# A graph-attention and mixture-of-experts kernel: the last batch of ten edge tiles becomes two batches, of six and of four

## The chip, the core and the metric

The kernel runs on one core of one Trainium2 chip. The metric is device time in microseconds (us) of one execution; the smaller the better. The core has five engines with a queue of instructions each: TensorE (PE, matrix products, with its weight loads shown as PEld), VectorE (DVE), ScalarE (ACT), GpSimd (POOL, here the issuer of indirect DMAs) and SyncE (SP, here the issuer of the plain DMAs). Each engine works its queue in order; semaphores make it wait for others. Sixteen DMA engines move data between HBM and the on-chip memory.

## The reference

The input is a graph of 6250 nodes (256 features each) and 100000 edges, sorted by destination. Two layers follow each other, each with a residual.

```python
x = x + gnn(layernorm(x), [src, dst], edge_attr_2, W_forward, W_reverse, attn)
x = x + ffn(layernorm(x), gate_w, gate_b, w1, b1, w2, b2)

# gnn: one message per edge, four heads, softmax over the edges of a destination
messages = h_fwd[src] * direction[:, 0:1] + h_rev[src] * direction[:, 1:2]
scores   = leaky_relu(einsum('ef,hf->eh', messages, attn))
norm     = exp(scores - max) / (segment_sum(exp(...), dst)[dst] + 1e-10)
out      = segment_sum(messages * norm, dst), for each head

# ffn: each token goes to the best of 8 experts (256 -> 1024 -> 256, relu), up to a capacity
idx  = argmax(softmax(x @ gate_w + gate_b));  pos = rank of the token within its expert
y    = expert(x)[idx, pos] * prob * (pos < capacity)
```

## The kernel before, in words

**Edges.** First a table of the nodes' products with the two weight matrices is written to HBM (node_tab). The 100000 edges make 782 tiles of 128 edges. The tiles are worked in batches of up to GB = 12 (two halves of GT = 6), in the order of the list `order` (L942): from the highest destination down to tile HEAD = 106, and at the end the 106 tiles of the head, which all belong to the first 128 nodes, upwards: eight batches of 12 and one of 10. That makes NB = 66 batches, numbered 0 to 65.

For each batch b:

- `gathers(b)` (L1041): POOL issues one indirect DMA per tile, which fetches the source rows into `gt` (three buffers). After the sixth tile it may put one waiting piece of POOL work (`pool_work`) between two gathers.
- `messages(b)` (L1051): DVE scales and adds the gathered rows (L1058 to L1067), makes scores (L1070), their maximum for the batch (L1074) and subtracts a shift (L1078); ACT takes the exponential (L1080).
- `places(b)` (L1083): DVE makes the 0/1 matrix `hot` (L1088) that says which of 128 destinations an edge has.
- `products(b)` (L1099): DVE multiplies messages by weights into `v` (L1103, L1104).
- `windows(b, half)` (L1117): PE adds six tiles at a time into the sums `pv` (two matmuls a tile, L1140). The 106 head tiles are summed in one `pv` without a break; after the last of them ACT copies the sums to `part_b` (L1144).

`hot`, `v`, `m` and `sc` have two buffers each. All of these and `gt` live in the pool p2.

**Routes.** The nodes are handled in 13 chunks (twelve of four tiles, the last one of the single tile 0). `route` (L1161) is a generator: once the edges of a chunk are summed, it finishes the attention, adds the residual, takes moments and normalises (L666 to L682), transposes on PE (L1201, `pt`), makes the logits (L1209, `pl`), picks the expert, counts positions with a matmul (L1231 and L1232, `pre`) and ends in `to_put` (L1256), the row to which each token is put. `put` (L1259, L1260) is the indirect DMA on POOL that writes the tokens into the experts' buffers `buf`. Early in a route the largest score so far is spread over the partitions with four transposes (`spread`, L1012 to L1017, `pm`), reduced by DVE (`over_s`) and put into the denominator.

**Experts.** Tokens are worked in four passes (`PASS`, 256, 384, 256 and 128 rows per expert); a pass can start once the chunks that belong to it are routed. The 32 jobs (24 of passes 0 to 2, then 8 of the last pass, numbered 24 to 31) form another generator, `experts` (L1385): transposes of the rows (`px`, L1335), products with the first weights (`ph`, L1409), with the second (`py`, L1426), bias and store (`y`, L1346, L1348). Rows, `w1t` and `w2t` are loaded on SP (L1320, L1297, L1305). Jobs 24 and 25 use the weights of jobs 22 and 23 again; those of 26 to 31 are fetched anew into the pool p6. The transposes of the next job come ahead of a job's `py` if that job's rows have been asked for (L1417).

**The order.** The whole order is written out by hand (manual schedule); each engine gets its instructions in the order in which the Python code issues them. The loop over b (L1505) runs NB + 1 times. Between the edge steps it takes expert steps: `step_experts(share)` (L1494) adds a half share (SHARE / 2 = 4.25) to a credit, then takes steps while the credit is positive, and each step takes off its cost, the number that the generator yields (0.86 for `px`, 1.72 for `ph`, 3.4 for `py`; the route's PE steps take off theirs as well). One turn of the loop is, in short:

```python
messages(b)
windows(b - 1, 0);  step_experts(SHARE / 2);  step_routing()
places(b);  step_routing();  products(b);  step_routing()
windows(b - 1, 1);  step_experts(SHARE / 2);  step_routing()
gathers(b + 3)
```

In turn NB - 2 the last chunk's loads are issued (L1513); in turn NB its route joins the list (L1519), so that it goes on at each `step_routing`. After the loop the pool p2 is closed and p6 takes its space (L1549, L1550). Then, in order: weights of job 26 (L1551); the rest of the last route, one step at a time, each followed by one expert step and one `fetch_and_finish` (L1555); the last put (L1559); the rows of jobs 24 and 25 and the weights of 27 and 28 (L1562 to L1566); the global check of the scores (L1571); then the expert steps that are left, with one `fetch_and_finish` after every second one (L1597); then what is left of `fetch_and_finish`, the last indirect stores, and a flag that says whether a general path has to be taken (L1610 to L1622).

`fetch_and_finish` (L1455) works on pairs of node tiles, 22 in all: it finishes the pair that was fetched four calls ago (L1374 on DVE, a store on SP, L659) and asks for the next pair (two indirect gathers `yg` on POOL, L1442, and `xr` on SP, L1446).

Of the kernel before, what the change touches and what calls it, by code (L numbers as in the profile page):

```python
# [519 lines left out]
def kernel(  # L520
# [50 lines left out]
    GB = 12  # L571

    def tiles_of(n, sign):

        u = (n / N) ** 0.5
        return (NE * u + sign * 5 * (NE * u * (1 - u)) ** 0.5) / P
# [3 lines left out]
    HEAD = int(tiles_of(P, -1)) // 2 * 2  # L580
    NL = (int(0.56 * ET) - HEAD) // GB
    GT = GB // 2
# [357 lines left out]

    assert TOP < ET and (TOP - HEAD) % GB == 0
    order = [(TOP, ET)] + [(i, i + GB) for i in range(TOP - GB, HEAD - 1, -GB)]  # L942
    order += [(i, min(i + GB, HEAD)) for i in range(0, HEAD, GB)]
    NB = len(order)
    done_at = [max(ROUTE_AT - 1, next(b for b, (i0, i1) in enumerate(order) if i0 <= groups[r][0])) for r in ready]
    done_at.append(NB - 1)
# [50 lines left out]
    with tc.tile_pool(name="p4", bufs=1) as p4, tc.tile_pool(name="p5", bufs=2) as p5, \  # L997
# [507 lines left out]
        for b in range(NB + 1):  # L1505
# [37 lines left out]
            if wait_pass and not pool_work:  # L1543
                taken["rows"] = wait_pass.pop() + 1
                i = (taken["rows"] - 1) * E
# [107 lines left out]
```

## Time and profile before

| | |
|---|---|
| median of 6 runs | 1281.58 us (1276.67 to 1283.38) |
| profiled execution | 1281.67 us, its span 1279.9 us, 14755 instructions |
| mean granted TensorE clock | 0.887 |
| PE busy | 1021.7 us (80% of the span) |
| DVE busy | 871.9 us (68%) |
| POOL busy | 864.3 us (68%) |
| ACT busy | 283.2 us (22%) |
| moved by DMA | 218.47 MB, mean 171 GB/s |
| last gather of an edge tile issued | 1136.1 us |
| last edge matmul ends, part_b is copied | 1161.4, 1161.9 us |
| the last put of the routes | 1180.1 us |
| rows of job 24 asked for | 1185.2 us |
| last expert matmul ends | 1267.1 us |

All times of single instructions count from the span's start. A line such as "PE L1140 MATMUL pv<-v,hot x12" is a run of twelve instructions of one source line; "[2.05 <-DMA xe<-buf]" says that the engine was idle for 2.05 us ahead of it and that a landing DMA ended this. In a list of waits the numbers are the total, how many times, and the longest. The shares of the whole span say little about a change at one place of a long order: the stretch in question has to be read by itself.

### The profile page before, as it was taken

The page shows a single profiled execution, that of the slowest core. Times are in us where ns is not written, and L with a number is a line of the kernel's source. Part 1 is how long each engine was busy: PE and PEld are TensorE (multiplying, and loading weights), DVE is VectorE, ACT ScalarE, POOL GpSimd, SP SyncE. Part 2 cuts the span into 40 slices and gives each one's busy share as a digit, 9 for nine tenths or more (in the row PEclk, how much of TensorE's full clock was granted, in tenths as well). Part 3 has the DMA queues.
Part 4 walks back from the last instruction along what each step waited for, and adds up shares of the span by engine and source line. Part 5 has one row for each costly group of instructions (what it writes and reads, how often), then busy time and mean ns, then how long its engine had stood idle before and what let it go on. Part 6 is the DMA issues. An engine that isn't in the chain of part 4 may idle for free.

```text
span 1279.9 us, 14755 instructions
## 1 busy us (share of the span) xinstructions
PE 1021.7 (80%) x4658; PEld 857.5 (67%) x4658; DVE 871.9 (68%) x1879; ACT 283.2 (22%) x754; POOL 864.3 (68%) x912
## 2 busy tenths in 40 slices
PE   4825555566749979797997997998999989999886
PEld 4814444455538768686876776776777878888775
DVE  6845666788828959686767768867786688664222
ACT  2510001121112232322122221222122112123222
POOL 2457777777767775767677777777777777744243
PEclk9966777677768888899998998998999999999988
DMA  8425555457355674757574663655455564646994
GB/s 273 131 69 133 140 137 143 117 135 248 105 149 172 173 216 139 216 142 203 149 217 115 183 174 98 182 148 157 142 143 156 150 207 114 202 157 243 333 378 138
DMA packets 154149, 218.47 MB, mean 171 GB/s; under 512 B 20198, under 2 KB 125963, under 8 KB 153933
## 3 DMA queue, kind: packets, MB, share of 16 engines
q1 hardware_dynamic: 121981, 142.51, 34.8%
q0 software_dynamic: 31440, 73.83, 23.3%
q10 hardware_dynamic: 640, 1.09, 0.2%
q8 instruction: 39, 0.64, 0.2%
q14 instruction: 49, 0.40, 0.1%
HBM read 160.50 MB, written 57.25 MB: 170 GB/s over the span
## 4 chain that ended last, share of the span: by engine, by line
PE 45%; DVE 18%; POOL 16%; DMA 10%; issue 8%; SPq 1%; ACT 1%; DVEq 0%; POOLq 0%; ACTq 0%
PE pv L1140 15%; POOL gt L1045 15%; PE py L1426 11%; PE ph L1409 10%; DVE v L1104 4%; DMA gt<-node_tab,srci 2%; PE pl L1209 2%; PE pn L814 2%; PE pv L1139 1%; DMA part<-sums 1%; PE pt L1201 1%; DMA buf<-hx,to_put 1%; DVE ln_st L671 1%; DVE m L1067 1%; DMA sums<-r 1%
## 5 line engine op out<-in xcount | busy, mean ns | idle before, releaser
L1045 POOL DMA_INDIRECT gt<-node_tab,srci x782 | 744.3, 952 | 246.2 <-issue 230.6
L1140 PE MATMUL pv<-v,hot 128*128 128x260 f32 x1564 | 437.0, 428 | 72.9 <-DVE v L1104 68.6
L1140 PEld LDWEIGHTS pv<-v,hot 128*128 128x128 f32 x1564 | 333.8, 217 | 139.1 <-issue 74.9
L1426 PE MATMUL py<-w2t,hf 128*128 128x256 f32 x1024 | 235.4, 384 | 0.3 <-DVE y L1346 0.3
L1409 PE MATMUL ph<-xT,w1t 128*128 128x256 f32 (+2 forms) x1024 | 234.8, 382 | 0.7 <-ACT xT L1336 0.7
L1104 DVE TENSOR_TENSOR v<-m,fixed 128x3072 f32<-128x3072 f32 (+1 forms) x66 | 218.7, 3313 | 2.3
L1426 PEld LDWEIGHTS py<-w2t,hf 128*128 128x128 f32 x1024 | 195.2, 193 | 26.9 <-DVE y L1346 0.6
L1409 PEld LDWEIGHTS ph<-xT,w1t 128*128 128x128 f32 x1024 | 176.8, 192 | 43.8 <-ACT xT L1336 1.1
L1412 ACT ACTIVATE hf<-ph,b1t 128x256 f32<-128x256 f32 (+2 forms) x256 | 108.1, 473 | 193.7 <-PE ph L1409 193.3
L1060 DVE TENSOR_TENSOR gt<-gt,fixed 128x816 f32<-128x816 f32 (+1 forms) x66 | 65.6, 994 | 102.7 <-DMA gt<-node_tab,srci 92.5
L1088 DVE TENSOR_TENSOR hot<-fixed,local 128x1536 f32<-128x1536 f32 (+1 forms) x66 | 114.1, 1729 | 0.2 <-PE pv L1140 0.2
L1346 DVE TENSOR_TENSOR y<-py,b2b 128x512 f32<-128x512 f32 (+1 forms) x40 | 23.3, 582 | 103.9 <-PE py L1426 103.9
L1442 POOL DMA_INDIRECT yg<-ybuf,to_get x44 | 42.0, 955 | 72.7 <-ACT part_b L1144 25.2
L1201 PE MATMUL pt<-ident,hx 128*128 128x128 f32 x98 | 22.6, 400 | 72.9 <-DVE hx L681 72.9
L1067 DVE TENSOR_TENSOR m<-gt,rv 128x408 f32<-128x408 f32 (+1 forms) x131 | 75.5, 576 | 4.5
L1065 DVE TENSOR_TENSOR rv<-gt,fixed 128x408 f32<-128x408 f32 (+1 forms) x131 | 76.1, 581 | 2.2
L1112 ACT COPY vl<-v 128x260 f32<-128x260 f32 x56 | 22.9, 408 | 224.0 <-DVE v L1104 101.1
L1080 ACT ACTIVATE v<-sc 128x48 f32<-128x48 f32 (+1 forms) x66 | 15.9, 242 | 254.6 <-DVE sc L1078 254.4
L1201 PEld LDWEIGHTS pt<-ident,hx 128*128 128x128 f32 x98 | 17.4, 206 | 78.2 <-DVE hx L681 28.4
L1260 POOL DMA_INDIRECT buf<-hx,to_put x49 | 49.5, 1010 | 28.6 <-issue 12.2
L1028 DVE TENSOR_REDUCE over_s<-pm 128x4 f32<-128x512 f32 x14 | 9.6, 688 | 53.6 <-PE pm L1016 53.6
L1148 ACT COPY r<-pv 128x260 f32<-128x260 f32 x86 | 31.8, 370 | 62.5 <-PE pv L1140 45.4
(206 smaller groups left out, 812.2 us busy)
## 6 DMA issues: line engine op xcount, KB each, us to landing
w1t<-in_L_ffn_w_dram SPq DMA_DIRECT2D x30, 1024.0 KB, 6.6
w2t<-in_L_ffn_w_dram SPq DMA_DIRECT2D x30, 1024.0 KB, 7.2
gt<-node_tab,srci POOLq DMA_INDIRECT x782
sums<-r SPq DMA_DIRECT2D x86, 130.0 KB, 2.1
buf<-zeros SPq DMA_DIRECT2D x16, 512.0 KB, 6.7
part<-sums SPq DMA_DIRECT2D x12, 520.0 KB, 6.1
ybuf<-y SPq DMA_DIRECT2D x24, 256.0 KB, 6.1
x_d<-hx SPq DMA_DIRECT2D x11, 512.0 KB, 3.0
```

What stands on the lines that cost most here:

```text
L1045: nc.gpsimd.indirect_dma_start(out=gts[b][:, i - i0, :], out_offset=None, in_=node_tab, in_offset=bass.IndirectOffsetOnAxis(ap=srci[:, i:i ...
L1060: nc.vector.tensor_mul(fw, fw, fac[:, 0, :n].unsqueeze(2).to_broadcast([P, n, MS]))
L1065: nc.vector.tensor_mul(rv[:, :k, :], gt[:, a0:a1, MS:ROW], fac[:, 1, a0:a1].unsqueeze(2).to_broadcast([P, k, MS]))
L1067: nc.vector.tensor_add(m[:, a0:a1, :], fw[:, a0:a1, :], rv[:, :k, :])
L1088: nc.vector.tensor_tensor(hot[:, :n, :], lane_p.unsqueeze(1).to_broadcast([P, n, P]), local[:, i0:i1].unsqueeze(2).to_broadcast([P, n, P]) ...
L1104: nc.vector.tensor_mul(v[:, :n, 0:H * O].rearrange("p n (h o) -> p n h o", h=H), m[:, :n, 0:O].unsqueeze(2).to_broadcast([P, n, H, O]), w[ ...
L1140: nc.tensor.matmul(pv, hot[:, i - i0, :], v[:, i - i0, :], start=(i == g0), stop=(i == g1 - 1))
L1201: nc.tensor.transpose(pt[:, q, d, :], h[:, n + q, d * P:(d + 1) * P], ident)
L1260: ins = nc.gpsimd.indirect_dma_start(out=bufs[p], out_offset=bass.IndirectOffsetOnAxis(ap=to_put[:, n0 + n:n0 + n + 1], axis=0), in_=hx[:, ...
L1409: nc.tensor.matmul(ph[:, f - f0, :], w1t[:, d, f * P:(f + 1) * P], xT[:, d, :S], start=(d == 0), stop=(d == DC - 1))
L1412: nc.scalar.activation(hf[:, f, :S], ph[:, f - f0, :], AF.Relu, bias=b1t[:, e * FC + f:e * FC + f + 1])
L1426: nc.tensor.matmul(py[:, j - j0, :], hf[:, f, j * P:(j + 1) * P], w2t[:, f, :], start=(f == 0), stop=(f == FC - 1))
```

## The change

The list `order` gets one entry more. Of the head's 106 tiles, the eight full batches stay; the last ten tiles, one batch (96, 106) before, become two, (96, 102) and (102, 106). NB becomes 67. The functions that work a batch are not touched; the two last batches have only a first half, so their second window returns at once (L1126).

```diff
     order = [(TOP, ET)] + [(i, i + GB) for i in range(TOP - GB, HEAD - 1, -GB)]
-    order += [(i, min(i + GB, HEAD)) for i in range(0, HEAD, GB)]
+    SHORT = (HEAD - 1) // GB * GB
+    order += [(i, i + GB) for i in range(0, SHORT, GB)]
+    order += [(i, min(i + GT, HEAD)) for i in range(SHORT, HEAD, GT)]
     NB = len(order)
```

What follows from NB moves with it: the loop has 68 turns in place of 67, with two calls of `step_experts` in each; the last chunk's loads are issued in turn 65 in place of 64, and its route joins in turn 67 in place of 66.

## Prediction

> **What bounds the kernel now.** I read the stages first (busy time by stretch), then the chain of waits, then the timeline of each engine around the edit. The edit touches only the last ten of 782 edge tiles, so only what follows about 1139 us can move.
>
> Stretches; columns: us, busy time and count of PE, PEld, DVE, ACT, POOL, then clock, DMA share, GB/s:
> ```profile
> 1140.00:1150.00 10.00, 10.00 (x50) 8.75 (x49) 7.64 (x12) 2.88 (x8) 0.00 (x0) 1.00 0.36 116
> 1150.00:1160.00 10.00, 10.00 (x50) 8.77 (x49) 0.20 (x1) 0.46 (x1) 0.00 (x0) 1.00 0.11 42
> ...
> 1162.00:1187.00 25.00, 22.39 (x112) 19.24 (x110) 14.20 (x70) 10.84 (x23) 17.16 (x18) 1.00 0.95 333
> 1187.00:1209.20 22.20, 18.13 (x116) 16.73 (x116) 5.16 (x22) 5.21 (x18) 4.17 (x5) 1.00 1.00 326
> 1209.20:1221.40 12.20, 9.15 (x51) 8.10 (x51) 2.67 (x13) 2.66 (x9) 5.11 (x7) 0.82 1.04 387
> 1221.40:1241.70 20.30, 17.73 (x101) 15.77 (x102) 5.38 (x26) 5.21 (x18) 8.13 (x9) 0.86 1.07 391
> 1241.70:1262.00 20.30, 20.30 (x138) 19.06 (x139) 7.29 (x36) 5.57 (x20) 15.24 (x17) 1.00 0.80 263
> ```
> Up to 1160 PE is full, while DMA idles and DVE has almost nothing left: the last edge tiles queue behind expert matmuls on PE. From 1162 the roles change: DMA is full for 80 us and PE waits.
>
> Waits from 1160 on (total, times, longest) and four pieces of the chain:
> ```profile
> POOL yg L1442 <- ACT part_b L1144: 25.2, 1, 25.2
> DVE over_s L1028 <- PE pm L1016: 12.8, 2, 11.8
> PE px L1335 <- DMA xe<-buf: 10.7, 4, 3.2
> ```
> ```profile
> 1159.76 1.75 PE pv L1140 x8
> ...
> 1180.06 5.13 DMA buf<-hx,to_put
> 1185.20 0.33 SPq L1320
> ...
> 1187.48 8.39 DMA w2t<-in_L_ffn_w_dram
> ```
> The switch is the end of the edges: the pool p6 (output rows, last weights) takes the space of the edge tiles, so POOL stood 25.2 us until the last edge matmul and its copy (part_b) were done. The second hinge is the one put of the last node tile: SP stood at xe<-buf until it had landed, and the weights of jobs 27 and 28 are issued behind that on SP.
>
> PE around the edit; numbers in brackets are idle time:
> ```profile
> 1153.08 2.79 PE L1140 MATMUL pv<-v,hot 128*128 128x260 f32 x12
> 1155.71 3.62 PE L1426 MATMUL py<-w2t,hf 128*128 128x256 f32 x16
> 1159.16 0.60 PE L1016 MATMUL pm<-ident,top_s 128*128 128x128 f32 x4
> 1159.60 1.92 PE L1140 MATMUL pv<-v,hot 128*128 128x260 f32 x8
> ...
> 1187.90 0.41 PE L1335 MATMUL px<-ident,xe 128*128 128x128 f32 x2 [2.05 <-DMA xe<-buf]
> ```
> The six tiles (x12) and the four (x8) stand one half share of expert work apart, and neither waits for its data.
>
> **Instructions added: about nothing.** Tiles, gathers (10) and matmuls (20) stay. The second batch adds eight DVE instructions (L1058, L1060, L1070, L1074, L1078, L1088, L1103, L1104) and one ACT (L1080, 0.24). Their fixed part comes from two shapes of one line: L1088 takes 1.749 for 1536 elements and 1.483 for 1280, so 0.15; L1104 (3.354, 2.822) gives 0.16. Eight times 0.16 is 1.3 us, in DVE's 11.81 us of idle ahead of over_s (without that cover: 1.3 us). The second batch's hot and v reuse the buffers of batch 64, free when its matmuls end at 1149.2; 0.7 and 1.2 us later they are ready, and PE wants them at 1164. The gt buffer has been free since 1114.6. The four pops of POOL work that leave with the split find an empty list now too (the last puts ran at 1083 to 1092).
>
> **Order moved: this is the cost.** One more turn of the loop puts two more half shares of 4.25 ahead of its end. I walked the credits (L1494, costs at the yields of L1385 on); both orders agree up to turn 66, where the credit is -1.08, and the walk of the old order gives the PE rows above. Old turn 66: W6, py (3.4), pm (0.9), W4, ph ph. New turn 66: W6, py, then 4.02 of credit buys ph ph ph; turn 67: W4, then 3.11 buys ph px py, then pm, then 0.48 buys one py. (W6, W4: the windows of six and four tiles.)
>
> Durations are those of the chain: py 3.45, three ph 5.18, one ph 1.73, px 0.44, pm 0.44, W4 1.75.
> 1. W4 ends at 1155.71 + 3.45 + 5.18 + 1.75 = 1166.1, before at 1161.35: the edges end **4.7 us later**. DMA, with share 0.11, has nothing to do in that time.
> 2. pm now stands behind ph px py: 1166.1 + 1.73 + 0.44 + 3.45 = 1171.7, before 1159.2. over_s to the add of part_b took 2.2 after it, and still does: 1173.9 (1161.96). The moments end 3.0 later, 1176.9. The table load for the root, which now ran at 1165.86 behind relus, has nothing ahead of it (at 1041.65 one ran 9 us ahead of its activation), so root, reciprocal and scaling take 1.1: PT at 1178.0 (1168.15), PE idle 0.7 (1.46).
> 3. The route's remaining steps fall between ph, ph, ph, py, py of job 23, where they fell between ph, px, py, py of 22: PL at 1180.0, PRE at 1183.8, to_put 2.3 after that: 1186.3 (1176.8). Job 23 ends at 1191.0.
> 4. POOL issues 14 output gathers at 1.25 ahead of the put, from 1167.0. The last pair needs the first pair's buffer: finished by DVE behind lg at 1182.7, its store lands 2.8 later, 1185.5, two gathers to 1188.1. The put goes at 1188.4 (1180.06); with the chain's 5.13 xe is issued at 1193.5. SP has its own way there: y of job 23 (0.7 after 1191.0), the third finish 0.8, two issues 0.9: 1193.4. Both say **8.3 us later** than 1185.2.
> 5. Old PE had py of job 23 in hand behind this px; the new order has done it. So PE stands from 1191.4 to 1196.2 (2.05 before), and ph of job 24 starts, after the copy of xT, at 1197.3 (1195.06): +2.2, if DMA let it run.
> 6. It doesn't. Weights 27 go at 1195.4 (1187.0). Of DMA's first block (25 us at 0.95, from 1167) 24 us are done at 1191, so it idles some 4 us more. From 1187 to 1242 it was full and moved 20.0 MB (364 GB/s) up to PE's last wait, px of job 29. In the new order two calls of fetch_and_finish (0.75 MB each, with gathers) and one y (0.26) no longer lie ahead of that px: 18.3 MB. At 364 that ends at 1195.4 + 50.2 = 1245.6, +3.9; at the 391 of 1221 to 1242 (46.8) at 1242.2, +0.5. If rows and stores moved there by no bytes at all, +8.4. I take **+3.0**, nearer to the full-stage rate than to the best slice, since the bytes left are the same mix.
> 7. The new order makes 23 fetch_and_finish calls inside the loops where 25 stood; 26 are needed. So three pairs, not one, stay behind the last y on DVE: 2 x 0.81 = **+1.6**, straight ahead of L1610, on the path. Bounds: 0 (if a wait for xr absorbs it) and 4 (if the last xr is late itself).
>
> Sum: 3.0 + 1.6 = +4.6 on the profiled execution's 1281.67 (span 1279.9, 1.8 around it): **1286.3**. The median shown is 1281.58, so the same holds for it.
>
> A rule beside step 6: the Trainium skill, "DMA: Bandwidth & Descriptors", Specifications, gives some 358 GB/s as one core's HBM limit and 435 as the fabric's ceiling. The trace's 391 over 20 us passes the first. By 358 the 18.3 MB end 4.8 us late (sum 1288.1), by 435 DMA never holds px and the sum is step 5 and 7 alone, 1285.5.
>
> **Rivals.**
> - *Full shift.* DMA stays the bound from weights 27 to the end, and moving rows behind weights saves nothing: 8.4 + 1.6 = +10, 1291.7. For it: share 1.00 to 1.07 for 55 us. Against: 0.80 afterwards, so bytes can move there.
> - *Not slower: DMA and the tail absorb it.* Two row fetches fewer ahead of the weights give 4 to 5 us, and PE's 10.7 us of px waits in the tail take the rest; step 6 becomes +0.5 or less, step 7 hides. It decides when DMA runs at 390 or more from 1195 on: 1283, with 1280.3 to 1284.3 around it. For it: 387 and 391 in two stretches; against: 326 in the first one.
> - *Earlier windows.* Six tiles need only six gathers, so they could start sooner. W6 at 1153.08 shows no idle time: PE is the one that is late, so this gives 0; with the 2.2 of step 5 not needed, 1277 to 1280.
>
> **Numbers.** Forecast (+2.6 to +7.6, 1284.3 to 1289.3) 0.50, of which 0.12 lies within 0.3%; full shift 0.17; absorbed 0.22; no cost or a gain 0.11, of which 0.05 beyond 0.3%. About 0.3% (3.8 us) is what a measurement can tell from no change here. Slower 0.38 + 0.17 = 0.55; same 0.12 + 0.22 + 0.06 = 0.40; faster 0.05. Range 1281 to 1292: some 0.15 lies below it (0.11 and the low end of "absorbed") and 0.03 above.
>
> **What would show it.** Step 1: POOL's first L1442 near 1167. Steps 2 to 4: three ph between W6 and W4, pm near 1171.7, put near 1188, xe near 1193.5. Step 5: one px wait near 5 us with no py behind it. Step 6: a dip in DMA share just before 1195, then weights 27; px of job 29 at 1242 to 1246. Step 7: three pairs of L1374 after the last y. I am wrong if the put goes before 1185 (then the first pair's buffer was no limit), or if the last px wait comes no later than now.

## The result and the profile after

The changed kernel takes 1286.6 us in the median of 20 runs (1280.5 to 1289.87), the kernel before 1279.1 in 46 runs (1274.55 to 1286.14). The ratio is **1.0055 [1.0044, 1.0067]**, about +7.0 us (1279.1 x 0.0055; 5.6 to 8.6 by the interval): slower, and by more than the 0.3% that a measurement can tell. The profiled execution took 1286.39 us with a span of 1284.7, granted clock 0.881 (0.887 before), 218.47 MB moved as before.

Two single executions can't be laid side by side by their clocks. The window of six tiles (W6) starts at 1153.08 in the trace before and at 1150.44 in the one after, and in the five experiments that are judged below, each of which differs from one of these two kernels only from W6 on, anywhere from 1145.2 to 1151.3. So all comparisons below count from the start of W6. From there to the end of the span it is 126.8 us before (1279.9 - 1153.08) and 134.3 after: +7.4, which agrees with the medians.

PE of the kernel after, around the edit (start, duration, what; idle time in brackets):
```profile
1150.44 2.79 PE L1142 MATMUL pv<-v,hot 128*128 128x260 f32 x12
1153.07 3.62 PE L1428 MATMUL py<-w2t,hf 128*128 128x256 f32 x16
1156.52 5.34 PE L1411 MATMUL ph<-xT,w1t 128*128 128x256 f32 x24
1161.70 1.92 PE L1142 MATMUL pv<-v,hot 128*128 128x260 f32 x8
1163.46 1.89 PE L1411 MATMUL ph<-xT,w1t 128*128 128x256 f32 x8
1165.18 0.60 PE L1337 MATMUL px<-ident,xe 128*128 128x128 f32 x4
1165.62 3.62 PE L1428 MATMUL py<-w2t,hf 128*128 128x256 f32 x16
1169.08 0.60 PE L1018 MATMUL pm<-ident,top_s 128*128 128x128 f32 x4
...
1196.23 0.66 PE L1337 MATMUL px<-ident,xe 128*128 128x128 f32 x2 [4.47 <-DMA xe<-buf]
```
This is the order of step 1: three ph stand between the two windows where pm stood, the window of four (W4) starts 11.3 us after W6 instead of 6.5, and pm comes after ph, px and py. (In this kernel the lines behind L944 stand two further down.)

Waits of the kernel after, 1160 to 1280 us (total, times, longest):
```profile
POOL yg L1444 <- ACT part_b L1146: 29.8, 1, 29.8
PE px L1337 <- DMA xe<-buf: 13.0, 5, 4.5
```
POOL stands 4.6 us longer for the edges to end, as step 1 wants it; and PE's waits for rows grew by 2.3 (10.7 before). The second is no measure of the loss: f1 below, which is not slower, has 13.1 us in five such waits.

The two kernels by four stretches: from W6 to the end of W4, the next 32 us, from there to the last wait of PE (px of job 29), and to the end. Columns: busy time and count of PE, PEld, DVE, ACT, POOL, then clock, DMA share, GB/s. First before:
```profile
1153.08:1161.35 8.27, 8.27 (x41) 7.22 (x40) 1.48 (x4) 0.20 (x1) 0.00 (x0) 1.00 0.08 16
1161.35:1193.35 32.00, 28.49 (x142) 24.67 (x141) 14.45 (x72) 11.59 (x25) 18.57 (x19) 1.00 0.95 331
1193.35:1241.67 48.32, 39.54 (x242) 35.72 (x240) 13.21 (x61) 12.71 (x44) 15.97 (x17) 0.89 1.04 369
1241.67:1279.90 38.23, 25.73 (x168) 23.67 (x168) 11.08 (x53) 7.76 (x27) 16.79 (x18) 0.89 0.50 167
```
Then after:
```profile
1150.44:1163.45 13.01, 13.01 (x61) 11.40 (x60) 1.23 (x2) 2.52 (x6) 0.00 (x0) 1.00 0.30 102
1163.45:1195.45 32.00, 25.45 (x127) 21.74 (x125) 15.25 (x72) 8.79 (x19) 17.16 (x19) 0.94 0.77 246
1195.45:1243.10 47.65, 37.85 (x234) 34.71 (x235) 11.57 (x58) 13.19 (x45) 13.30 (x14) 0.89 1.07 375
1243.10:1284.70 41.60, 27.49 (x168) 25.05 (x168) 12.41 (x61) 7.75 (x27) 20.73 (x22) 0.83 0.59 189
```
Read the last two columns. The third stretch is nearly the same in both: DMA full, 48 us. The first two are not: the first is 4.7 us longer with DMA busy for less than a third of it, and in the second DMA falls from 331 to 246 GB/s. The fourth is 3.4 us longer.

In bytes (the DMA view of the same stretches): before 0.14, 10.59, 17.83 and 6.38 MB, after 1.33, 7.88, 17.86 and 7.88 MB, in sum 34.94 and 34.95. If the rate of a full DMA is put at 375 GB/s (that of the third stretch after), the time that is not paid for by bytes, up to px of job 29, is:

- before: 88.6 us - 28.56 MB / 375 = 88.6 - 76.2 = **12.4 us**
- after: 92.7 us - 27.07 MB / 375 = 92.7 - 72.2 = **20.5 us**

So DMA lost 8.0 us more, and 4.0 of it came back since 1.49 MB less had to pass ahead of that px. This leaves +4.1 at the px of job 29 (92.66 - 88.59). Put at 360 or at 391 GB/s, the two losses differ by 8 us as well. The other 3.3 up to the end come behind it and are taken apart in the point on step 7.

### The profile page after: what moved, and what is told of

Read it like the earlier page. It is cut to its first block, busy times and chain, and to the rows that moved or that the text cites. A ratio compares the mean times of both kernels' runs of the same rounds, so it can differ in the third digit from the quotient of the medians.

```text
span 1284.7 us, 14766 instructions
## 1 busy us (share of the span) xinstructions
PE 1021.9 (80%) x4658; PEld 858.5 (67%) x4658; DVE 871.6 (68%) x1887; ACT 283.9 (22%) x755; POOL 863.3 (67%) x912
## 2 busy tenths in 40 slices
DMA packets 154149, 218.47 MB, mean 170 GB/s; under 512 B 20198, under 2 KB 125963, under 8 KB 153933
## 4 chain that ended last, share of the span: by engine, by line
PE 57%; DVE 14%; POOL 12%; DMA 7%; issue 6%; SPq 1%; ACT 1%; DVEq 0%; POOLq 0%; ACTq 0%
PE pv L1142 20%; PE py L1428 14%; PE ph L1411 14%; POOL gt L1047 11%; DVE v L1106 3%; DMA out_dram<-yg 3%; PE pn L814 2%; PE pv L1141 2%; PE pl L1211 2%; DMA gt<-node_tab,srci 2%; DVE ln_st L671 1%; PE pt L1203 1%; DVE part L1189 1%; DVE hx L1190 1%; PE px L1337 1%
## 5 line engine op out<-in xcount | busy, mean ns | idle before, releaser
L1414 ACT ACTIVATE hf<-ph,b1t 128x256 f32<-128x256 f32 (+2 forms) x256 | 108.2, 473 | 194.6 <-PE ph L1411 194.4
L1337 PE MATMUL px<-ident,xe 128*128 128x128 f32 x128 | 21.8, 285 | 31.0 <-DMA xe<-buf 31.0
```

Of the source, the lines that this page charges most:

```text
L1414: nc.scalar.activation(hf[:, f, :S], ph[:, f - f0, :], AF.Relu, bias=b1t[:, e * FC + f:e * FC + f + 1])
```

## Experiments

None of these kernels leaves out or changes any of the computation. Eight different kernels were run, four of them twice: in the first and the third batch (labels with e and g) the kernel before itself took 1764.55 and 1784.9 us, and in the trace of e1 the engines wait for something outside what the profile shows ("remote": ACT alone 211.2 us in 23 waits ahead of L1414, the longest 36.4). The intervals there are wider than what was looked for, so those batches settle nothing, and only the five kernels of the other two batches (labels with f and h), beside which the kernel before ran at 1279.24 and 1279.9 us, are judged.

**e1 and f1: the second batch, but the old order.** The ten tiles stay split; the half shares and route steps that the extra turn of the loop brings are skipped (the diff is cut: the route steps behind places and products are put under `if b != NB` in the same way, the one behind the second window under `if b != NB - 1`).

```diff
-            step_routing()
+            if b != NB:
+                step_routing()
...
-            if b == NB:
+            if b == NB - 1:
                 routing.append(last_chunk)
...
                 windows(b - 1, 0)
-            step_experts(SHARE / 2)
-            step_routing()
+            if b != NB:
+                step_experts(SHARE / 2)
+            if b != NB:
+                step_routing()
...
-            step_experts(SHARE / 2)
+            if b != NB - 1:
+                step_experts(SHARE / 2)
```

> Two batches of six and four tiles as in the changed kernel, but the added turn of the loop gets no expert shares of its own and the last route joins one turn earlier, so that PE's order of work is that of the kernel before, instruction by instruction. Order theory (the loss comes from the expert steps put ahead of the last four tiles and of the last route): as fast as before, ratio 1.000 within 0.002, edges' end, put and rows of job 24 where they were (1161, 1180, 1185). Batch theory (the loss comes from the second batch itself: eight more DVE instructions, smaller gathers, its buffers): 1.0055 against before, as the changed kernel.

e1: 1767.45 against 1764.55, 1.0027 [0.9963, 1.0091]: inconclusive.

> The split kernel with the order of the kernel before, once more, since the first measurement ran at 1765 us for the kernel before, with gathers that took far longer, and its intervals are wider than the effect. Order theory: ratio 1.000 within 0.002 against the kernel before. Batch theory: 1.0055.

f1: 1280.17 against 1279.24, **1.0015 [0.9996, 1.0034]**. No loss is left that this can tell; the interval leaves room for one of 0.34%, but does not meet that of the changed kernel (1.0044 to 1.0067). PE of f1, split and yet with py and pm between its windows:
```profile
1147.50 2.79 PE L1142 MATMUL pv<-v,hot 128*128 128x260 f32 x12
1150.13 3.62 PE L1428 MATMUL py<-w2t,hf 128*128 128x256 f32 x16
1153.59 0.60 PE L1018 MATMUL pm<-ident,top_s 128*128 128x128 f32 x4
1154.02 1.92 PE L1142 MATMUL pv<-v,hot 128*128 128x260 f32 x8
```

**e4 and f4: one batch of ten, but the new order.** The counterpart, made from the kernel before: in turn NB two more half shares, the window of four between them, and the route steps of that turn behind them.

```diff
                 windows(b - 1, 0)
             step_experts(SHARE / 2)
-            step_routing()
             if b < NB:
+                step_routing()
                 places(b)
-            step_routing()
+                step_routing()
             if b < NB:
                 products(b)
+            if b == NB:
+                step_experts(SHARE / 2)
+                windows(b - 1, 1)
+                step_experts(SHARE / 2)
+                step_routing()
+                step_routing()
             step_routing()
-            if b:
+            if b and b < NB:
                 windows(b - 1, 1)
```

> The batch of ten stays whole as in the kernel before, and two half shares of expert work are added in the last turn, one ahead of the last four tiles, one behind them and ahead of the score spread; PE's order is that of the changed kernel. Order theory: ratio 1.0055 within 0.002 against before, put near 1188, a wait of 4 to 5 us ahead of px of job 24. Batch theory: 1.000.

e4: 1765.8 against 1764.55, 1.0021 [0.9958, 1.0084]: inconclusive.

> The whole batch of ten with PE's order of the changed kernel, once more for the same reason. Order theory: ratio 1.0055 within 0.002, put 27 to 29 us after the last four tiles end (18.7 in the kernel before, 25.3 in the changed one), a wait of 4 to 5 us ahead of px of job 24. Batch theory: 1.000.

f4: 1284.7 against 1279.24, **1.0047 [1.0024, 1.0069]**: the loss of the change, without the change. Its first two stretches, as above:
```profile
1149.18:1162.20 13.02, 13.02 (x61) 11.40 (x60) 1.22 (x2) 2.51 (x6) 0.00 (x0) 1.00 0.33 102
1162.20:1194.20 32.00, 25.56 (x128) 21.83 (x127) 15.20 (x70) 8.78 (x19) 17.55 (x19) 0.94 0.77 251
```
They are those of the changed kernel almost digit for digit (13.01 us at 102, 246 GB/s after it). f1 and f4, measured side by side, lie 4.5 us apart in their medians. Together they show that the order which the extra turn brings, of the expert steps and with them of the last route's, makes the loss, and that the second batch itself costs nothing that could be measured.

**e2 and e3: one of the two half shares each.** From the changed kernel; e2 leaves out the second half share of turn NB - 1 (the ph between the windows), e3 the first one of turn NB (ph, px, py ahead of pm).

```diff
 e2:
-            step_experts(SHARE / 2)
+            if b != NB - 1:
+                step_experts(SHARE / 2)
 e3:
-            step_experts(SHARE / 2)
+            if b != NB:
+                step_experts(SHARE / 2)
```

> The split kernel without the half share that stood between the six tiles and the four; the two half shares of the last turn stay. The edges end when they did before (W4 straight behind py, about 5 us earlier than in the changed kernel), and the spread of the scores comes 6.9 us later than before (12.5 in the changed kernel). Pool theory (what costs is only that the pool p6 is free 4.7 us later): 1.000 against before. Route theory (what costs is the last route and the put behind it): put 5 to 6 us later than before, +3 us, ratio 1.0025.

> The split kernel without the first half share of the last turn, so that the spread of the scores follows the four tiles at once; the half share ahead of the four tiles stays. The spread comes at the same time as in the run without the other share, and the end of the edges 5.2 us later. Pool theory: 1.004 to 1.0055 against before, clearly above that run. Route theory: 1.0025 to 1.003, within 0.1% of that run, since POOL's gathers have until 1182 to end.

1777.99 and 1777.42 against 1764.55: 1.0083 [1.0014, 1.0152] and 1.0095 [1.0036, 1.0153], in a batch where neither e1 nor e4, which has the whole of the new order, could be told from the kernel before (1.0027 and 1.0021). How the loss divides between the two half shares stays open.

**f6: the weights of 27 and 28 ahead of the route.** If the late put delays the loads behind it on SP, then loads that need no put should not stand behind it.

```diff
-        fetch_w1(LP + 2)
-        fetch_w2(LP + 2)
+        for i in more:
+            fetch_w1(i)
+            fetch_w2(i)
         while routing:
...
-        for i in more[1:]:
-            fetch_w1(i)
-            fetch_w2(i)
```

> The changed kernel with the weights of jobs 27 and 28 asked for on SP together with those of 26, as soon as the edges end, ahead of the put and of the rows of job 24. Step 6 (DMA is the bound from the weights of job 27 on; it lost about 6 of the 24 us between the end of the edges and the put): those idle stretches carry 4.2 MB, 11 us of DMA, so the last px wait on rows goes and PE comes at it 8 to 11 us earlier: ratio 0.998 to 1.000 against the kernel before. Rival (the late px of job 24 alone costs, 2 to 5 us on PE, and weights are never late): 1.0055 as the changed kernel, or above it, because rows queue behind weights.

1286.79 against 1279.24, **1.0076 [1.0054, 1.0099]**: no gain over the changed kernel, and the expectation that it would recover the loss fell. SP and a wait of f6:
```profile
1160.99 6.59 SPq L1299 DMA_DIRECT2D w1t<-in_L_ffn_w_dram  x1
...
1170.82 5.10 SPq L1350 DMA_DIRECT2D ybuf<-y  x1
1175.96 4.50 SPq L1448 DMA_DIRECT2D xr<-x_d  x4
```
```profile
POOL yg L1444 <- DMA xr<-x_d: 15.7, 1, 15.7
```
The six weight loads, 1 MB each, are asked for within 11 us. The issue of the fifth took 6.59 us and that of the y behind them 5.10, where 0.34 to 0.4 is usual; the small xr loads that DVE's finishes need come behind them, and DVE waited 10.9 us for them (1.3 in the changed kernel). POOL then stands 15.7 us ahead of its last two gathers, and the put goes 33.8 us after W4's end (25.3 in the changed kernel, 18.7 before). The bytes of the first 32 us rose to 9.78 MB, but the time in which DMA has too little to do came later: 323 GB/s from there up to px of job 29, 375 in the changed kernel.

**g1 and h1: the put as soon as its rows are known.** In the changed kernel the put waits behind the last pair of gathers on POOL. Here it goes ahead of them, and the loads of rows and weights with it; the same lines behind the loop go.

```diff
         while routing:
             step_routing()
+            if todo:
+                for do in pool_work + todo:
+                    do()
+                del pool_work[:], todo[:]
+                taken["released"] = taken["rows"] = NP
+                fetch_rows(LP)
+                fetch_rows(LP + 1)
+                for i in more[1:]:
+                    fetch_w1(i)
+                    fetch_w2(i)
             step_ffn()
             fetch_and_finish(3)
-        for do in pool_work + todo:
...
```

> The changed kernel with the last put issued as soon as its row number is there (ahead of the sixth and seventh fetch_and_finish), and the rows of jobs 24 and 25 and the weights of 27 and 28 straight behind it on SP. The edges end when they do in the changed kernel. Put theory (the late put holds SP and with it the weights, DMA idles meanwhile): put 5 us earlier (20.3 us after the end of the last four tiles in place of 25.3), weights 27 some 4 us earlier, px of job 29 some 3.7 us earlier, ratio 1.002 to 1.003 against the kernel before. Pool theory (only the later end of the edges, when p6 becomes free, costs): no gain, 1.0055.

g1: 1792.64 against 1784.9, 1.0041 [0.9995, 1.0088]: inconclusive.

> The changed kernel with the put and what follows it ahead, once more, since the kernel before ran at 1785 us beside the first measurement. Put theory: put 20.3 us after the last four tiles end (25.3 in the changed kernel), weights 27 some 4 us earlier, ratio 1.002 to 1.003 against the kernel before, and as many px waits as in the kernel before. Pool theory (only the later end of the edges costs): 1.0055.

h1: 1287.15 against 1279.9, **1.0067 [1.0045, 1.009]**. The put goes 20.6 us after W4's end (1184.90 - 1164.27) where it went at 25.3; the weights of 27 go 38.5 us after W6's start (1189.80 - 1151.26), 43.5 in the changed kernel. And nothing is gained. PE at the two px, and the 32 us after the edges, in h1:
```profile
1191.22 0.44 PE L1337 MATMUL px<-ident,xe 128*128 128x128 f32 x2 [1.43 <-DMA xe<-buf]
...
1211.77 0.66 PE L1337 MATMUL px<-ident,xe 128*128 128x128 f32 x2 [6.68 <-DMA xe<-buf]
```
```profile
1164.27:1196.27 32.00, 29.49 (x149) 25.82 (x148) 14.79 (x68) 9.28 (x21) 14.26 (x15) 0.95 0.77 242
```
The wait at px of job 24 shrank from 4.47 to 1.43 and came back as 6.68 at job 26. This stretch goes with it: 242 GB/s, as in the changed kernel (246). The weights came earlier, but stores, xr loads, two gathers and a y went behind them, so in the 32 us after the edges the same bytes were moved, 7.73 and 7.88 MB. The explanation that the put's time alone makes the loss fell here.

**g2 and h2: the mirror image.** If two half shares more cost 7 us, do two less give anything? From the kernel before, both half shares of the last turn are left out; their steps come after the loop. The edit stands behind both windows.

```diff
-            step_experts(SHARE / 2)
+            if b != NB:
+                step_experts(SHARE / 2)
```

> The mirror of the change: the kernel before (one batch of ten) without the two half shares of expert work in the loop's last turn, so that the last four tiles and the score spread follow the six tiles at once. Order theory: the edges end 3.5 us earlier, the put about 4 us earlier (POOL's 14 gathers are ahead of it), weights 27 as well, one more call of fetch_and_finish inside the loops: ratio 0.996 to 0.998 against the kernel before. Rival (PE is short of expert work in the tail only by what DMA brings, or PE loses what it gains while it waits for the route): 1.000.

g2: 1783.15 against 1784.9, 1.0017 [0.9974, 1.006]: inconclusive.

> The mirror (the kernel before, without expert shares in the loop's last turn), once more for the same reason. Order theory: edges end 3.5 us earlier, put about 4 us earlier, ratio 0.996 to 0.998 against the kernel before. Rival (PE loses while it waits for the route what it gains later, or DMA's bytes alone set the end): 1.000.

h2: 1279.71 against 1279.9, **1.0007 [0.9989, 1.0024]**: no gain. The edges end 3.5 us sooner after W6 (4.81 us instead of 8.27), and px of job 24 does not wait. But the wait comes back two jobs later; PE of h2 at px of job 26:
```profile
1208.17 0.66 PE L1335 MATMUL px<-ident,xe 128*128 128x128 f32 x2 [5.63 <-DMA xe<-buf]
```
By the sum used above h2 wastes less DMA time than any other kernel (91.95 us - 30.26 MB / 375 = 11.3 us). But expert steps that stood in the loop now stand behind it, and calls of fetch_and_finish between them: 1.7 MB more than before pass ahead of px of job 29 (4.5 us at 375 GB/s), which comes 3.4 us later after W6. Something is saved behind that: the flag's matmul (L1617) starts 5.7 us after the last py begins, 6.8 before, so fewer finishes are left after the last y.

**g3: both of the last two** (g2's edit and g1's, on the kernel before).

> The mirror and the early put together, on the batch of ten. Order and put theory: put 6 to 7 us earlier than before, ratio 0.994 to 0.997 against the kernel before. If DMA's bytes alone set the end once it is full (the rows moved behind the weights come back later), no better than the mirror alone.

1786.87 against 1784.9, 1.0035 [0.9993, 1.0077], in the third batch: inconclusive.

The kernels that are judged, from W6's start, in us and MB; "lost" is the time to px of job 29 less its bytes at 375 GB/s:

| | order of steps | put after W4's end | px 29 | MB up to it | lost | end of the span | ratio |
|---|---|---|---|---|---|---|---|
| before | old | 18.7 | 88.6 | 28.56 | 12.4 | 126.8 | 1 |
| f1 | old, split | 20.7 | 90.7 | 28.53 | 14.6 | 130.8 | 1.0015 |
| h2 | mirror | 22.8 | 92.0 | 30.26 | 11.3 | 129.3 | 1.0007 |
| f4 | new, unsplit | 25.1 | 93.2 | 27.25 | 20.5 | 135.9 | 1.0047 |
| after | new | 25.3 | 92.7 | 27.07 | 20.5 | 134.3 | 1.0055 |
| h1 | new | 20.6 | 93.6 | 27.10 | 21.3 | 134.3 | 1.0067 |
| f6 | new | 33.8 | 95.0 | 27.25 | 22.3 | 135.1 | 1.0076 |

The three kernels that lose 11 to 15 us can't be told from the kernel before, the four that lose 20 to 22 are slower; the time of the put does not sort them (20.6 in h1, 20.7 in f1). Each row is one execution: f1 has the same order on PE as the kernel before and ends 4.0 us later after W6, of which 2.1 are there at px of job 29 and 1.7 come right behind it, at a lower granted clock, though its median over the runs is within 1 us of it. So differences of a few us between two rows can't be read, and the table shows that the lost time goes with the order, not that it is the whole of the cause.

## Why the prediction was right, and where it was not

**Size.** 1286.3 was forecast and 1286.6 measured, but the times meet more closely than the differences do. The baseline's median over more runs is 1279.1, not 1281.58. As a difference, +4.6 was forecast and +7.0 (5.6 to 8.6) measured. That the two times are 0.3 us apart is luck: a baseline 2.5 us lower makes up for a difference that was forecast 2.4 us too small.

**Instructions added, about nothing: right.** f1 has them all and is at 1.0015, with 1 inside its interval.

**Step 1: right to the tenth.** W4 ends 13.01 us after W6's start, as 1166.1 - 1153.08 says; f4 shows the same number without the split.

**Steps 2 and 3: right.** pm starts 18.64 us after W6's start (18.6 forecast), PE idles 0.70 ahead of pt (0.7 forecast), and pre starts 31.0 us after W6's start (1181.44; 30.7 forecast).

**Step 4: too short by 3 us, and one queue was missed.** The put goes at 1188.77, 38.3 us after W6's start (35.3 forecast; 27.0 before). SP of the kernel after, and a wait on it:
```profile
1176.04 0.34 SPq L1350 DMA_DIRECT2D ybuf<-y  x1
1176.43 2.03 SPq L1448 DMA_DIRECT2D xr<-x_d  x4
```
```profile
SPq L1350 <- DVE y L1348: 15.1, 2, 11.4
```
The store of a job's y stands ahead of the xr loads on SP and waited 11.4 us, because DVE does that y behind the route's normalisation. So the four xr loads went 13.0 us after W4's end; in the trace before they went 1.9 us after it:
```profile
1163.23 4.31 SPq L1446 DMA_DIRECT2D xr<-x_d  x4
```
DVE's first finish waited 1.3 us for them, and POOL idled 7.2 ahead of the last pair. The working looked at SP only for the y of job 23. DVE's wait is the smaller part of the 3 us: the store of that first finish was issued at 1181.51, and the next gather went 4.8 us later (1186.27), where the working had 2.8 for the store to land. What made it longer isn't shown; the profile names no releaser for this gather. From the put to the rows it then took 3.4 us instead of the 5.13 of the old chain, and the rows were asked for 9.6 us later than before (8.3 forecast).

**Step 5: the wait's size was right, its place and its cost were not.** One wait of 4.47 (4.8 forecast) at px of job 24, with no py behind it. But that px comes 45.8 us after W6's start (43.1 forecast): its rows were asked for 1.3 us later than forecast and took 4.1 us from the issue to px where the working had 2.7, and PE had stood 2.16 us already ahead of the global check's pm. So ph of job 24 starts 5.0 us later than before, not 2.2.

**Step 6: the bytes were right, the size was short, and the cause was put at the wrong place.** From the weights of 27 (1193.95) to px of job 29, 18.35 MB were moved (18.3 forecast) at 374 GB/s. At its two rates the working had +0.5 and +3.9 (and +8.4 if no bytes moved behind px) and took +3.0; measured is **+4.1**. Its parts: W6 to W4 takes 4.7 longer; DMA falls behind by 1.52 MB more up to 32 us after that (10.73 MB from W6 on before, 9.21 after), which is 4.1 us at 375; 0.8 comes back in the third stretch; 4.0 are saved by 1.49 MB less. The sum is 4.7 + 4.1 - 0.8 - 4.0 = 4.0, the measured 4.1 but for rounding. The "some 4 us more" of idle DMA were right in size, then, but the working had them in one place, just ahead of the weights of 27. In the trace after there are two thin places: 156 GB/s from 24 to 28 us after W6's start, where the xr loads had stood behind the y on SP until 26.0 (217 before), and 184 and 171 in the two times 4 us from 32 to 40, ahead of the put (247 and 358 before). What was wrong is the link from step 4: that the put holds the weights of 27 and these hold px of job 29. h1 brought both forward by about 5 us and px of job 29 did not come earlier (93.6 after W6, 92.7 in the changed kernel). That the size still came out near is in part luck. With the late end of the edges, DMA has too little to do in the 32 us after it, in the changed kernel and in h1 alike; in f6, where weights filled them, it had too little to do later. Why it can't be filled up is not shown.

The rule weighed beside this step, 358 GB/s for one core (the Trainium skill, "DMA: Bandwidth & Descriptors", Specifications), is passed again: 374 GB/s over 49 us.

**Step 7: right.** The flag's matmul (L1617) starts 8.18 us after the last py begins (1274.59 - 1266.41), 6.79 before: +1.4, forecast +1.6. In the chain of the kernel after, three pairs stand ahead of the check for finite values and the flag, where one stood (the first line is of the kernel before):
```profile
1268.17 0.82 DVE yg L1374 x4
...
1271.47 2.12 DVE yg L1376 x11
1273.62 0.20 DVE finite L1612
```
f1 has 6.79 here and f4 8.18, so this too goes with the order.

**What no step had.** Between px of job 29 and the last py, 23.31 us pass instead of 21.76, since py of job 28 ran at a lower granted clock:
```profile
1243.55 4.96 PE L1428 MATMUL py<-w2t,hf 128*128 128x256 f32 x16
```
It took 3.62 before, but 5.31 in f1, which has the old order, 6.34 in f4, and 3.62 in f6 and h1, which have the new one. So these 1.5 us are not shown to come from the change. The three slow ones follow waits of 3.0 to 3.5 us at px of job 29, but h1 waited 3.4 there and ran its py in 3.62, so the wait alone does not decide it. With them the execution is complete: 4.1 + 1.5 + 1.4 + 0.4 behind the flag = 7.4.

**The rivals.** *Full shift* (+10) did not come: moving 1.5 MB past px of job 29 did save 4 us, by the sum above. *Absorbed* had its condition stated as 390 GB/s or more from 1195 on; it was 374. *Earlier windows* did not show: PE has no idle time ahead of W6 in the trace after.

**Open.** What would fill DMA in those 32 us without a loss later was not found. The xr loads behind the y on SP are a candidate, from the trace alone; moving them ahead of that store was not tried. Nor is it settled which of the two half shares costs how much (e2, e3). No version here beats the kernel before.

## What to carry to other kernels

Where a loop hands out other work by turns, splitting one item gives the loop one more turn, and the work of that turn lands ahead of whatever ends the stage; count it with the loop's own credits before the split's benefit is counted. Where the engines change roles at one event (here the space that the last edge tiles give free), look at what a delay of that event leaves idle on the engine that is the bound afterwards. Here a delay of 4.7 us went with a loss, an event 3.5 us sooner (h2) gained nothing, and both tries at moving transfers forward behind it (f6, h1) only moved the wait. Add up bytes and time of the whole stretch from that event to the last wait: here the idle time of the bound, and not the time of the put, told the slower kernels from the others.

## What was not expected of the hardware

One issue on SP takes 0.38 us when little is queued, but 4.5 us behind some 4 MB of weights (the store at 1198.93 in the kernel after) and 6.59 behind 4 MB in f6. Small transfers behind large ones pay twice, in the issue and in landing: that store landed 11.65 us after its issue began, where one such store took 2.8 us in the kernel before (issued at 1173.97). And the granted clock in the 22 us after px of job 29 was 1.00 in four of seven executions and 0.88 to 0.93 in three, with both orders in either group.
